# Planned transfer times, fewer reserved buffers, first transfers in pieces and a joint ending of the last two batches, in a fused four-layer graph network

## The chip, the core and the metric

The kernel runs on one NeuronCore of one Trainium2 chip. The metric is the device time of one execution, in microseconds (us), as the median of several executions. Each kernel was timed beside runs of the kernel before on the same chip. A ratio in this text is the mean time of one kernel's fast runs over that of the other's of the same rounds, so it is not quite the ratio of the medians that are quoted.

## The reference

For each of 32 batches there are 512 nodes of 128 features (`x`) and a dense 512x512 adjacency matrix (`adj`). Four residual graph layers follow each other, each behind a layer norm and a relu:

```python
h = relu(layernorm(x)); x = x + L0(h, adj)   # degree-normalised convolution, leaky relu
h = relu(layernorm(x)); x = x + L1(h, adj)   # in and out aggregation, node term, tanh
h = relu(layernorm(x)); x = x + L2(h, adj)   # four stacked layers, adj l2-normalised by rows / by columns
h = relu(layernorm(x)); x = x + L3(h, adj)   # message, aggregation, GRU-like gates
```

Everything is f32. PE (TensorE) does the products. All batches are independent, so work of one batch can fill the waits of another.

## The kernel before

The kernel describes each batch as a list of operations with an estimated duration, and a planner written in Python puts all operations of all batches into one order per engine. It is a list scheduler: an operation's key is its batch's due time minus the length of the chain that still follows it, and a buffer is only given to a younger batch if enough stay free for each older one (`kept`). The order is fixed when the kernel is built. On the chip each engine works strictly in that order.

```python
PERIOD = 20.0
...
    def order(self):
        ...
            o.tail = max([o.us + o.land] + [self.lag(o, n) + n.tail for n in o.next if n.batch == o.batch])
            o.key = (o.batch * PERIOD - o.tail, i)
        ...
                    older = item[1].batch - min(unfinished)
                    if any(len(free[x.kind]) < len([...]) + older * self.kept.get(x.kind, 0) for x in new):
                        held.append(item)
                        continue
...
    plan = Plan(sb, psum, {"bank": 8, "s2": 32, "s4": 6, "s8": 10}, {"bank": 1, "s2": 5, "s4": 1, "s8": 2})
...
        # transfers have fixed landing times in the plan
        op("SP", 0.1, lambda: nc.sync.dma_start(a.ap(), adj[b]...), [], [a], land=5.3)
```

The kind `s8` holds the large matrices: the adjacency `a`, its transpose `aT`, and a second copy `aT2` for the last layer, 1 MB each, and the last layer's gates `g`.

A norm goes through four engines. VectorE makes the moments, GpSimd the power -1/2, VectorE the bias `nb`, ScalarE the normalised relu `h`; PE then transposes `h`, and the next layer starts from that:

```python
            op("POOL", 0.35 + 0.17 * n, lambda: nc.gpsimd.tensor_tensor(inv..., v8..., neg_half..., op=ALU.pow), ...)
            op("DVE", 0.16, ... nb = -mean * inv ...)
            for c in range(NC):
                op("ACT", t_act(D, 2), ... h[c] = relu(inv[c] * x[c] + nb[c]) ...)
        ...
                op("PE", 0.11, lambda c=c: nc.tensor.transpose(ps..., h.ap()[:, c, :], ident), ...)
```

The l2 factors of the third layer are computed per node on partitions, written to DRAM (`bounce`) and read back as rows on all partitions (`rows`); eight multiplies on VectorE then scale `a` and `aT`.

## Time and profile before

| what | kernel before |
|---|---|
| time | 2486.97 us median of 3 (2486.08 to 2491.35) |
| span of the profiled run, mean granted clock | 2485.6 us, 0.992 |
| PE busy | 97% |
| a batch every (distance of adjacency loads) | 75.5 us |
| idle of PE between 300 and 2300 us, in the list of waits | 10.6 us |

One more view is needed later: PE's waits in the stretch from 300 to 2300 us (columns: who waited, for whom, us in total, times, the longest).

```profile
PE ps_agg L267 <- DVE sd L418: 8.7, 19, 0.6
```

This is nearly all that the list shows. It says that the aggregations of the third layer sometimes wait for VectorE's addition `sd`, and that PE hardly waits for anything else.

### The profile page before, as it was taken

The numbers are of one execution on the slowest core, as the hardware profiler recorded it, in microseconds if no ns is written. First come the engines' busy times: TensorE is split into PE (matmuls) and PEld (weight loads), VectorE is DVE, ScalarE is ACT, GpSimd is POOL, SyncE is SP. The second block draws the span as 40 slices with busy tenths as digits, with TensorE's granted clock in tenths as the row PEclk, the third lists the DMA queues.
The fourth block names the chain that finished last, engine by engine and source line by source line (L and its number), as shares of the span: only waits on it lengthen the run. The fifth ranks groups of instructions, "written<-read, shape, count | busy, mean of one in ns | idle before, by whom it ended". The sixth has DMA issues, their size and how long they took to land. (4 is left out here: it accounts for less than half of the span.)

```text
span 2485.6 us, 23454 instructions
## 1 busy us (share of the span) xinstructions
PE 2419.9 (97%) x8898; PEld 1466.4 (59%) x8898; DVE 1136.9 (46%) x2832; ACT 744.0 (30%) x1633; POOL 253.7 (10%) x199
## 2 busy tenths in 40 slices
PE   5899999999999999999999999999999999999997
PEld 4556566556566556566565665565665666655654
DVE  5334455444454444454444554444544444544343
ACT  3221333332333322333322333223333223333121
POOL 1110111100011101011101111010111010110000
PEclk8999999999999999999999999999999999999998
DMA  8011111111112111122111121111111121211000
GB/s 245 20 51 51 64 35 64 66 58 51 51 51 64 60 51 64 35 68 64 60 51 64 34 64 60 55 59 51 51 64 59 51 64 35 68 51 64 13 5 9
DMA packets 123489, 139.67 MB, mean 56 GB/s; under 512 B 36592, under 2 KB 69360, under 8 KB 123376
## 3 DMA queue, kind: packets, MB, share of 16 engines
q1 hardware_dynamic: 122368, 134.36, 16.9%
q10 hardware_dynamic: 1008, 3.81, 0.4%
q8 instruction: 70, 1.15, 0.2%
q14 instruction: 43, 0.35, 0.1%
HBM read 129.64 MB, written 8.52 MB: 56 GB/s over the span
## 5 line engine op out<-in xcount | busy, mean ns | idle before, releaser
L267 PE MATMUL ps_agg<-aT,sd 128*128 128x512 f32 x1024 | 504.5, 595 | 10.5 <-DVE sd L418 9.9
L267 PEld LDWEIGHTS ps_sd<-w_sb,f 128*128 128x128 f32 x1792 | 335.0, 190 | 252.9 <-issue 186.3
L267 PE MATMUL ps_sd<-w_sb,f 128*128 128x256 f32 x1792 | 482.0, 381 | 0.8 <-ACT f L541 0.8
L267 PE MATMUL ps_agg<-a,sd 128*128 128x512 f32 x1024 | 479.0, 592 | 0.0
L363 POOL TENSOR_TENSOR sc<-v,neg_half 128x4 f32<-128x4 f32 (+1 forms) x128 | 150.0, 1172 | 1933.7 <-DVE v L430 1046.8
L541 ACT ACTIVATE f<-ps_agg,cf_sb 128x512 f32<-128x512 f32 x128 | 88.0, 687 | 768.6 <-PE ps_agg L267 767.1
L418 DVE TENSOR_TENSOR sd<-ps_sd,rf_sb 128x512 f32<-128x512 f32 x256 | 175.9, 687 | 309.7 <-PE ps_sd L267 309.7
L267 PEld LDWEIGHTS ps_agg<-a,sd 128*128 128x128 f32 x1024 | 187.4, 190 | 195.8 <-issue 194.2
L375 ACT ACTIVATE h<-xr,nb,sc 128x128 f32<-128x128 f32 x384 | 158.1, 482 | 366.8 <-DVE nb L371 366.8
L267 PEld LDWEIGHTS ps_agg<-aT,sd 128*128 128x128 f32 x1024 | 189.4, 190 | 129.9 <-issue 92.8
L267 PE MATMUL ps_agg<-f,w_sb 128*128 128x512 f32 x448 | 228.7, 593 | 0.0
L429 DVE TENSOR_REDUCE stat<-a 128x4 f32<-128x2048 f32 x32 | 73.1, 2286 | 312.1 <-DMA a<-in_adj 312.1
L267 PE MATMUL ps_agg<-aT,rep 128*128 128x512 f32 x256 | 134.9, 609 | 4.2 <-DVE rep L481 4.2
L267 PE MATMUL ps_agg<-a,rep 128*128 128x512 f32 x256 | 132.0, 597 | 0.0
L267 PE MATMUL ps_agg<-aT,msg 128*128 128x512 f32 x256 | 124.0, 595 | 1.1 <-DVE msg L558 1.1
L525 DVE TENSOR_TENSOR a<-a,rows 128x512 f32<-128x512 f32 x128 | 116.5, 911 | 5.0 <-PE ps_agg L267 3.3
L575 DVE TENSOR_TENSOR g<-ps_gate,r_sb 128x512 f32<-128x512 f32 x128 | 79.5, 683 | 78.4 <-PE ps_gate L267 78.4
L267 PEld LDWEIGHTS ps_gate<-w_sb,hT 128*128 128x128 f32 x512 | 89.6, 193 | 36.0 <-issue 29.7
L267 PE MATMUL ps_gate<-w_sb,hT 128*128 128x256 f32 (+1 forms) x512 | 104.6, 329 | 0.0
L418 DVE TENSOR_TENSOR sd<-ps_sd,r_sb 128x512 f32<-128x512 f32 x64 | 44.2, 691 | 131.4 <-PE ps_sd L267 131.4
L456 DVE SCALAR_TENSOR_TENSOR z<-ps_lin,sc,r_sb 128x128 f32<-128x128 f32 x128 | 36.2, 343 | 143.4 <-PE ps_lin L267 143.3
L267 PE MATMUL ps_agg<-aT,h 128*128 128x256 f32 (+2 forms) x384 | 100.8, 384 | 0.0
(90 smaller groups left out, 2657.5 us busy)
## 6 DMA issues: line engine op xcount, KB each, us to landing
aT<-in_adjt SPq DMA_DIRECT2D x64, 1024.0 KB, 5.4
a<-in_adj SPq DMA_DIRECT2D x32, 1024.0 KB, 5.4
rows<-bounce SPq DMA_DIRECT2D x32, 512.0 KB, 4.4
x<-in_x SPq DMA_DIRECT2D x32, 256.0 KB, 2.8
out<-xo SPq DMA_DIRECT2D x32, 256.0 KB, 2.3
raw<-in_raw ACTq DMA_DIRECT2D x2, 768.0 KB, 9.6
w_sb<-in_w ACTq DMA_DIRECT2D x2, 448.0 KB, 6.8
r_sb<-in_brow ACTq DMA_DIRECT2D x1, 704.0 KB, 6.0
```

The costliest lines, as they stand in the source:

```text
L267: op("PE", t_mm(n), lambda: nc.tensor.matmul(out_of(ps.ap()), lhs(), rhs(), start=start, stop=stop), reads, [(ps, part) if part is not Non ...
L363: op("POOL", 0.35 + 0.17 * n, lambda: nc.gpsimd.tensor_tensor(inv.ap()[:, :n], v8.ap()[:, :n], neg_half[:, :n], op=ALU.pow), [v8, NH], [(i ...
L375: op("ACT", t_act(D, 2), lambda c=c: nc.scalar.activation(h.ap()[:, c, :], xin.ap()[:, c, :], AF.Relu, bias=nb.ap()[:, c:c + 1], scale=inv ...
L418: op("DVE", t_tt(N), lambda ps=ps, h=h: nc.vector.tensor_add(sd.ap()[:, 2 * h:2 * h + 2, :], ps.ap().rearrange("p (j v) -> p j v", j=2), a ...
L429: op("DVE", 2.2, lambda: nc.vector.tensor_reduce(stat.ap(), a.ap(), AX.X, ALU.add), [a], [stat])
L456: op("DVE", 0.28, lambda c=c: nc.vector.scalar_tensor_tensor(z.ap()[:, c * D:(c + 1) * D], ps0.ap()[:, c * D:(c + 1) * D], inv0.ap()[:, NC ...
L525: op("DVE", t_tt(N), lambda m=m, c=c, s=s: nc.vector.tensor_mul(m.ap()[:, c, :], m.ap()[:, c, :], rows.ap()[:, s, :]), [(m, {c}), rows], [ ...
L541: op("ACT", t_act(N, 1), lambda ps=ps, i=i, f_new=f_new: nc.scalar.activation(f_new.ap(), ps.ap(), AF.Tanh, bias=cf_sb[:, i:i + 1]), [ps, ...
L575: op("DVE", t_tt(N), lambda ps=ps, c=c: nc.vector.tensor_add(g.ap()[:, c, :], ps.ap(), r_sb[:, R_L3_G:R_L3_G + 4 * D]), [ps, RS], [(g, {c})])
```

## The change

Its intent, part by part:
1. The plan knows transfers by their size: each occupies its queue for kb/240 us and lands 1.3 us later, instead of fixed landing times.
2. The first transfers go in a fixed order (`rank`) and batch 0's matrices in four pieces, so that the first norm, row sums and aggregation can start early.
3. One `s8` buffer is kept per older batch instead of two.
4. `bounce` is stored with contiguous words; `rows` then comes back interleaved, and the multiplies read it with a stride of eight words.
5. Batch 31 is due 6 us after batch 30 instead of 20, so that the last two end together, and their gates go in chunks of 128 columns with two steps on GpSimd. The gate formula gets two ScalarE steps more and keeps six VectorE passes.

```diff
+ENDING = 6.0
+    RATE, TRANSFER = 240.0, 1.3
-    def op(self, engine, us, emit, reads=(), writes=(), land=0.0):
+    def op(self, engine, us, emit, reads=(), writes=(), kb=0.0, rank=None):
+        if kb:
+            o.us, o.land = max(us, kb / self.RATE), self.TRANSFER
-            o.key = (o.batch * PERIOD - o.tail, i)
+            due = o.batch * PERIOD if o.batch < B - 1 else (B - 2) * PERIOD + ENDING
+            o.key = (due - o.tail if o.rank is None else o.rank - 1e6, i)
-    plan = Plan(sb, psum, {... "s8": 10}, {"bank": 1, "s2": 5, "s4": 1, "s8": 2})
+    plan = Plan(sb, psum, {... "s8": 10}, {"bank": 1, "s2": 5, "s4": 1, "s8": 1})
...  (weights, biases and raw blocks: split, ranked, kb= instead of land=)
-        op("SP", 0.1, lambda: nc.sync.dma_start(a.ap(), adj[b]...), [], [a], land=5.3)
+        pieces = NC if b == 0 else 1
+        load(a, adj[b], 1024, 1)          # `pieces` transfers, rank 1 for batch 0
+        load(aT, adjt[b], 1024, 4)
...  (row sums and GpSimd's diagonal blocks follow the pieces of batch 0)
-        bounce, rows = buf("bounce", (2 * NC, P)), buf("s4", (P, 2, N), "rows")
+        bounce, rows = buf("bounce", (P, 2 * NC)), buf("s4", (P, P, 2, NC), "rows")
-        op("SP", 0.1, bounced, [inv], [bounce], land=4)
+        op("SP", 0.4, bounced, [inv], [bounce], kb=128)
+                    ... rows.ap()[:, :, s, :].rearrange("p n k -> p k n") ...   # stride of 8 words
+        at_end = b >= B - 2
+        side, side_engine = (nc.gpsimd, "POOL") if at_end else (nc.vector, "DVE")
+        w2 = 1 if at_end else NC
+            ... u, u, n = tanh(u), w = .5 - .5 z, q = .5 + .5 z, q *= h, q += x, n *= w, xo = q + n ...
```

## The prediction

> **What bounds the kernel now.** I read the page first: TensorE (PE) is busy for 97% of the span, in every slice but the first two and the last. Then I asked for PE's busy time in stretches (columns: stretch, its length, busy us and instructions, granted clock, DMA share, GB/s).
>
> ```profile
> span 2485.6 us, 23454 instructions
> PE 2419.9 (97%) x8898; PEld 1466.4 (59%) x8898; DVE 1136.9 (46%) x2832; ACT 744.0 (30%) x1633; POOL 253.7 (10%) x199
> ```
>
> ```profile
> 0.00:10.00 10.00, 0.00 (x0) 1.00 0.79 279
> 10.00:20.00 10.00, 6.17 (x32) 1.00 1.05 389
> 20.00:30.00 10.00, 7.41 (x36) 0.83 1.08 359
> 30.00:40.00 10.00, 7.37 (x37) 0.83 0.59 163
> 40.00:60.00 20.00, 14.11 (x41) 0.67 0.74 140
> 60.00:81.00 21.00, 14.67 (x57) 0.91 0.20 58
> ...
> 1300.00:2300.00 1000.00, 991.26 (x3651) 1.00 0.17 56
> 2300.00:2455.54 155.54, 155.23 (x571) 1.00 0.03 9
> 2455.54:2485.60 30.06, 13.65 (x56) 0.74 0.03 9
> ```
>
> See three kernels in one: a start of 81 us short of work and at a low clock, a long full middle, and a tail of 30 us that runs one batch's chain alone.
>
> How much PE work is there at full speed? In the timeline of the middle a product of 512 columns starts 0.86 us after the last, one of 256 after 0.43, of 128 after 0.22, a transpose after 0.11 to 0.12. One batch has 52, 40 and 28 such products, 3.5 us of mixed first-layer ones and 16 transposes: 44.7 + 17.2 + 6.2 + 3.5 + 2.0 = 73.6 us. With some 7 us of weight folding, 32 batches need 2362 us; 124 of the 2486 are lost. Where:
> - Start: PE's order and the timeline say that at 81 us it had done 33 us of work. Lost: 48.
> - End: from 2455.54 (last second-stack aggregation done) one batch's tail remains, 10.5 us of work in 30. Lost: 19.5.
> - Middle: the rest, 56, or 1.8 us a batch. The busy column hides most of it in pipelined ends; the distance between successive starts shows it. It agrees with the period: adjacency loads at 225.12 and 2263.61 us are 27 batches apart, 75.5 us each.
>
> The start, in the timeline: the first layer waits for data that all arrive together.
>
> ```profile
> 11.54 6.19 PE L267 MATMUL ps_fold<-raw 128*128 128x128 f32 x32 [11.54 <-DMA raw<-in_raw]
> 11.79 2.29 DVE L429 TENSOR_REDUCE stat<-a 128x4 f32<-128x2048 f32 x1 [4.56 <-DMA a<-in_adj]
> 18.66 0.87 DVE L347 BATCH_NORM_STATS2 bn<-x 128x6 f32<-128x128 f32 x4 [4.38 <-DMA x<-in_x]
> 45.20 3.78 PE L267 MATMUL ps_sd<-w_sb,hT 128*128 128x256 f32 x8 [0.68 <-ACT hT L386]
> 54.22 2.04 PE L267 MATMUL ps_agg<-aT,rep 128*128 128x512 f32 x2 [3.23 <-DVE rep L481]
> ```
>
> x, only 256 KB and the head of the chain, is used at 18.7 us, although a lone x load takes 2.6. Batch 0 reaches its second layer at 45.2. The last gates, in VectorE's timeline:
>
> ```profile
> 2474.15 2.48 DVE L575 TENSOR_TENSOR g<-ps_gate,r_sb 128x512 f32<-128x512 f32 x4 [7.93 <-PE ps_gate L267]
> 2477.33 0.69 DVE L583 SCALAR_TENSOR_TENSOR u<-g 128x512 f32<-128x512 f32 x1 [0.70 <-ACT g L580]
> ...
> 2481.68 0.69 DVE L590 TENSOR_TENSOR xo<-xr,dl 128x512 f32<-128x512 f32 x1
> ```
>
> PE ends at 2474.8; the span ends 10.8 later: 7.6 of VectorE and ScalarE in turn, 2.3 of output transfer, 0.9 of closing.
>
> **What the Trainium skill says.**
> 1. "TensorE: Matmul & The Clock Gate", section "What's actually happening": the array runs at half clock until it has been busy for about 3.4 us, and drops back after an idle window. The trace agrees: 0.67 to 0.91 granted in the hungry start, 0.74 in the tail, 1.00 between. So a wait costs more than its length, and a fuller tail is also a faster one.
> 2. "DMA: Bandwidth & Descriptors", section "Rules for kernel authors": a non-contiguous last dimension becomes one descriptor per element. The `bounce` store (4 KB as single words) takes 10.3 us median to land in the middle, against 2.3 for a 256 KB output: it agrees.
> 3. The same page, "Issuing engines are not separate DMA queues": all run on the same 16 engines and interleave. The window of 10 to 20 us shows 389 GB/s at a DMA share of 1.05: order and bytes decide, not queues.
> 4. "Vector Engine (DVE) Microarchitecture Reference", section "5.2 Measured stream behaviour on trn2 (trn3 not measured)": a source that hops at every element costs 1.73 ns a column instead of 1.05, up to 2.5 for small steps. No run so far shows it.
>
> **The change, part by part.**
>
> *First transfers.* Issued now: x, a in four pieces, small weights and biases beside them, then raw0, aT in four pieces, the rest. I lay them out at the measured 390 to 400 KB/us from about 2.2 us: x near 4 us; a with all before it is 1.45 MB, 6 us; raw0 7.8; aT 8.4 to 10.4; weights 12.8; the other raws 14.3 and 16.3; batch 1's a 19, aT 22.
>
> Chain of batch 0 with the trace's durations: last row sum 6.9, power on GpSimd (1.65) 8.9, two small VectorE steps 9.4, h from 9.9; the first aggregation behind the six raw0 folds (cold, 0.43 each), partly cold itself, about 10.8 to 16.5; copy and 4 products to 18.5; then z, y, residual, moments with fold copies between (5.5), power 1.1, h 1.7, transposes and copy 1: second layer at about **28.5** instead of 45.2. But PE has then done 10.7 us of work, not 15.5, since batch 1 comes later. Lost: 17.8 against 29.7, a gain of 12. From there to 81 us the old kernel lost another 18: cold products between 45 and 60, 3.2 for rep (a 2.28 us row sum of another batch stands before it), 2.6 for agg_in, 2.7 and 0.9 for the next norm. The new order keeps nearly all of these waits for a lone batch 0; I give it 5 us, mostly the row sum, which now comes before. **Start: -17.**
>
> *The middle.* The gate formula keeps six VectorE passes and adds two ScalarE ones, 1.2 us a batch on an engine 30% busy: nothing. `bounce` should land in about 2 us instead of 10, but no engine waited for rows: nothing. The eight multiplies by `rows` (680 and 691 ns) read every eighth word; by point 4 an estimate of 1.0 to 1.4 us each, some 4 us a batch on an engine 46% busy, and they precede the upd addition, which waits about 3.5 us after the aggregation anyway: up to 2 us hidden or spilt once.
>
> What matters is the new order (one kept buffer instead of two, other load times). I counted, in both kernels' PE order, the places where a result's first use follows its last producing product with less than 1.0 us of other work, about what an eviction takes: 5 a batch before (agg_in, agg_out, two hT, f), 2.5 after, total shortfall 0.74 and 0.36 us a batch. Times 31 that is 12 us; for slower multiplies and waits of norm chains, which this count does not see, I take a third off. **Middle: -8.**
>
> *The end.* Batch 31 is now due 6 us after batch 30 instead of 20. In the new order their last aggregations are 7 products apart; after the later one two tails remain, 20.5 us of work, where one (10.5) did. I walked it from that point, T0: f 1.8, h of batch 31 by 8.3, its message behind batch 30's gates at about 13.7, VectorE free after batch 30's four gate additions at 16, aggregation 16.4 to 19.8, gates to 23.3.
>
> Then the chunked ending: the order lists all four g additions, then 4 + 4 + 4 + 4 steps of 128 columns, so it is phased, not a true pipeline; ScalarE has 20 small pieces. By 0.22 to 0.28 us a step (the 128-column z steps: 1.13 for four) about 6 us, issue, 2 landing, closing: 9.3 instead of 10.8. End at T0 + 32.6, of which 20.5 is work: 12 lost instead of 19.5. **End: -7.5.**
>
> Sum: -17 - 8 - 7.5 = -32.5; 2487 - 32 = **2455 us**.
>
> **The rivals.**
> - *The end gives more, the start too: over 2%.* Needs 50 us, that is 40 of the 67.5 lost at both ends with 10 from the middle. For it: x can be there 14 us sooner and the tail was nearly idle. Against: every step of batch 0's chain between arrivals stays, alone and partly cold; two tails still hang on VectorE. Then 2430 to 2437.
> - *The plan breaks in the middle.* Rows' strided reads take 1.4 us, VectorE, which works in a fixed order, is late for the sd additions, whose slack is 1.07 to 1.28 us, and PE waits 0.3 to 0.5 more per batch instead of less: +10 to 15 us. For it: such a wait of 0.4 us per batch stands in the trace already. Against: in the new order no sd addition lies among the eight. Then 2470 to 2478.
> - *First transfers are hidden anyway.* If folds or the cold clock set the first 80 us, an earlier x is not worth 12 us: 2467. Against: folds are 7 us of 81.
>
> **Range and chances.** Start 10 to 24, middle -2 to 16, end 4 to 11; independent, they add to about 32 with 16 either way: 2439 to 2471. Over 2% faster is below 2437, just outside: 0.1. Over 2% slower needs +50 us, against three gains: 0.01.
>
> **What would show it.** Start: x statistics near 4 us, second-layer products near 28.5 (above 36 and the step is wrong); full busy windows from about 65. Middle: period 75.2, `rows` multiplies 1.0 to 1.4 us, bounce near 2 us, fewer waits for agg_in, agg_out, hT. End: last aggregation to end of span 32.6, PE end to end of span 9.3, clock near 1.0. The number is wrong if the period moves by more than 0.5 us in either direction, since it counts nearly thirty times.

## The result, and the profile after

The changed kernel took 2521.40 us (2520.69 to 2521.87, 4 runs) beside 2487.30 of the kernel before (2486.08 to 2491.35, 4 runs): a ratio of 1.0134 with a 95% interval of 1.0116 to 1.0152. It is 1.3% slower. That is still "within 2%", but far outside the predicted range of 2439 to 2471, and on the other side of the old time.

The page after, first lines (engine, busy us, share of the span, instructions):

```profile
PE 2422.4 (96%) x8898; PEld 1461.2 (58%) x8898; DVE 1218.1 (48%) x2855; ACT 786.8 (31%) x1719; POOL 363.0 (14%) x218
```

PE has the same number of products and the same busy time as before, in a longer span. VectorE has 81 us more and GpSimd 109 more. The same stretches as in the prediction, again with PE's busy time (columns: stretch, its length, busy us and instructions, granted clock, DMA share, GB/s):

```profile
10.00:20.00 10.00, 8.91 (x47) 1.00 1.04 400
20.00:30.00 10.00, 6.04 (x50) 0.97 1.01 329
...
40.00:60.00 20.00, 16.56 (x60) 0.84 0.61 204
60.00:81.00 21.00, 18.58 (x54) 0.84 0.24 76
...
1300.00:2300.00 1000.00, 972.11 (x3578) 1.00 0.17 55
...
2486.94:2519.90 32.96, 21.83 (x109) 0.92 0.06 17
```

The start is fuller, and the last row, which begins where the last second-stack aggregation is done, holds 21.83 us of work in 32.96 where the old tail held 13.65 in 30.06. Both ends do what they were meant to. The middle does not: 972 of 1000 us busy, where it had been 991. The steps of the start, in the timeline:

```profile
4.31 0.87 DVE L376 BATCH_NORM_STATS2 bn<-x 128x6 f32<-128x128 f32 x4 [4.31 <-DMA x<-in_x]
11.09 2.93 PE L276 MATMUL ps_fold<-raw 128*128 128x128 f32 x12 [11.09 <-DMA raw<-in_raw]
31.65 3.78 PE L276 MATMUL ps_sd<-w_sb,hT 128*128 128x256 f32 x8 [0.68 <-ACT hT L415]
39.71 2.05 PE L276 MATMUL ps_agg<-aT,rep 128*128 128x512 f32 x2 [2.95 <-DVE rep L516]
```

Batch 0 reaches its second layer 13.6 us sooner and the next aggregation 14.5 us sooner than before. PE's waits in the middle (300 to 2300 us, columns as above):

```profile
PE ps_t L412 <- ACT h L404: 29.1, 46, 0.9
PE ps_agg L276 <- DVE rep L516: 17.9, 25, 0.9
PE ps_agg L276 <- DVE sd L447: 4.9, 15, 0.3
```

Two waits have grown from nothing and from one wait of 0.8 us: the transposes for the normalised `h`, and the second layer's aggregation for `rep`. The old one, for `sd`, has become smaller.

**What a batch loses.** The list of waits and the busy columns miss whatever lies inside the modelled end of a product. So take the distances between successive starts on PE over the 27 batches between two loads of `a` (225.12 to 2263.61 us before, 207.6 to 2293.0 after), and subtract for each instruction the distance at which such instructions follow each other when nothing holds them up: 0.43 us for 512 columns (a product counts as two instructions), 0.32 for 384, 0.215 for 256, 0.111 for 128 and 0.11 for a transpose. What is left is lost time, here in us per batch by what comes next:

| lost, us per batch | before | after |
|---|---|---|
| at the transposes of `h` (before, inside or behind them) | 0.65 | 2.39 |
| at the aggregation of `rep` | 0.10 | 0.91 |
| at third-layer aggregations (`sd`) | 0.61 | 0.33 |
| at products of `hT` | 0.47 | 0.07 |
| everything else | 0.29 | 0.23 |
| sum | 2.12 | 3.93 |
| a batch every, from the adjacency loads | 75.50 | 77.24 |

The work of a batch is 73.4 us before and 73.3 after (the edges of the stretch are not quite alike), so the difference of the sums, 1.81, is that of the periods, 1.74, to within 0.1. So the change lost about 50 us in the middle (28 full batches by 1.74 are 49), and gained some 15 at both ends. Told apart by norm, the 0.65 of before lies wholly at the norm behind the first layer. After, all three transposed norms lose: about 1.1 us behind the first layer, 1.2 behind the second layer's update and 0.5 behind the third layer (these overlap a little with other rows).

**Where the new waits come from.** The chain in front of a late transpose, in the timeline of all engines after. PE's last update product ends at 1334.35, where its next one starts:

```profile
1321.49 1.27 POOL L472 TENSOR_TENSOR diag<-aT,ident 128x512 f32<-128x512 f32 x1 [5.01 <-ACT rep L513]
1321.66 1.40 DVE L514 TENSOR_SCALAR rep<-rep 128x512 f32<-128x512 f32 x1
...
1324.20 1.10 PE L276 MATMUL ps_agg<-aT,rep 128*128 128x512 f32 x2 [0.91 <-DVE rep L516]
...
1334.55 0.69 DVE L529 TENSOR_TENSOR u<-ps_upd,r_sb 128x512 f32<-128x512 f32 x1 [0.55 <-PE ps_upd L276]
1335.27 0.63 ACT L531 ACTIVATE y<-u 128x512 f32<-128x512 f32 x1 [3.35 <-DVE u L529]
1335.94 0.69 DVE L533 TENSOR_TENSOR xr<-xr,y 128x512 f32<-128x512 f32 x1
1336.66 0.87 DVE L376 BATCH_NORM_STATS2 bn<-xr 128x6 f32<-128x128 f32 x4
...
1338.16 1.01 POOL L392 TENSOR_TENSOR sc<-v,neg_half 128x4 f32<-128x4 f32 x1 [2.65 <-DVE v L379]
1339.40 1.65 ACT L404 ACTIVATE h<-xr,nb,sc 128x128 f32<-128x128 f32 x4 [2.00 <-DVE nb L400]
1339.95 0.71 PE L412 MATMUL ps_t<-ident,h 128*128 128x128 f32 x2 [0.69 <-ACT h L404]
```

Read it from 1334.35: update added, tanh, residual, moments, power, `h`, and the transpose at 1339.95, that is 5.6 us of chain. PE's other work in that time (four msg products of 0.111, ten instructions of 0.43) is 4.74, so PE stands for 0.86. The first three lines show the other wait: VectorE's scaling of `rep` takes 1.40 us, where the same instruction 1.4 us later takes 0.39, because GpSimd's diagonal addition runs beside it; the aggregation of `rep` waits for 0.91.

The same place in PE's timeline of the kernel before:

```profile
1156.34 1.02 PE L383 MATMUL ps_t<-ident,h 128*128 128x128 f32 x3
1157.19 1.02 PE L267 MATMUL ps_agg<-aT,msg 128*128 128x512 f32 x2
...
1173.60 1.02 PE L267 MATMUL ps_agg<-f,w_sb 128*128 128x512 f32 x2
...
1182.26 0.60 PE L383 MATMUL ps_t<-ident,h 128*128 128x128 f32 x4
```

Here the last update product ends at 1173.60 and the transposes stand at 1182.26, 8.66 us later. The chain has 3 us to spare. Over the whole middle, this distance is 8.66 to 8.88 us before, and 5.6 and 5.9 in turn after. The first two lines show a hidden wait of before: three transposes, 0.33 us of work, take 0.85 until the next start, though no idle time is noted in the brackets.

### The profile page after: what moved, and what is told of

The parts are those of the page before. It is cut to its first block, busy times and chain, and to the rows that moved or that the text cites. A ratio compares the mean times of both kernels' runs of the same rounds, so it can differ in the third digit from the quotient of the medians.

```text
span 2519.9 us, 23554 instructions
## 1 busy us (share of the span) xinstructions
PE 2422.4 (96%) x8898; PEld 1461.2 (58%) x8898; DVE 1218.1 (48%) x2855; ACT 786.8 (31%) x1719; POOL 363.0 (14%) x218
## 5 line engine op out<-in xcount | busy, mean ns | idle before, releaser
L276 PE MATMUL ps_sd<-w_sb,f 128*128 128x256 f32 x1792 | 466.5, 381 | 0.7 <-ACT f L415 0.7
L544 POOL TENSOR_TENSOR inv<-stat,neg_half 128x8 f32<-128x8 f32 x32 | 140.8, 4400 | 139.6 <-DVE stat L543 127.8
L560 DVE TENSOR_TENSOR a<-a,rows 128x512 f32<-128x512 f32 x128 | 151.7, 1186 | 1.1 <-PE ps_agg L276 1.1
L412 PEld LDWEIGHTS ps_t<-ident,h 128*128 128x128 f32 x384 | 52.6, 140 | 152.9 <-ACT h L404 130.5
L560 DVE TENSOR_TENSOR aT<-aT,rows 128x512 f32<-128x512 f32 x128 | 138.4, 1081 | 0.0
L621 ACT ACTIVATE g<-g 128x512 f32<-128x512 f32 (+1 forms) x68 | 40.9, 604 | 306.8 <-DVE g L611 306.8
L412 PE MATMUL ps_t<-ident,h 128*128 128x128 f32 x384 | 92.5, 297 | 40.7 <-ACT h L404 36.9
```

The source lines that it names most:

```text
L276: op("PE", t_mm(n), lambda: nc.tensor.matmul(out_of(ps.ap()), lhs(), rhs(), start=start, stop=stop), reads, [(ps, part) if part is not Non ...
L412: op("PE", 0.11, lambda c=c: nc.tensor.transpose(ps.ap()[:, c * P:(c + 1) * P], h.ap()[:, c, :], ident), [(h, {c}), ID], [(ps, {c})])
L544: op("POOL", 1.7, lambda: nc.gpsimd.tensor_tensor(inv.ap(), stat.ap(), neg_half, op=ALU.pow), [stat, NH], [inv])
L560: op("DVE", t_tt(N), lambda m=m, c=c, s=s: nc.vector.tensor_mul(m.ap()[:, c, :].rearrange("p (k n) -> p k n", k=NC), m.ap()[:, c, :].rearr ...
L621: op("ACT", t_act(cols), lambda s=s: nc.scalar.activation(g.ap()[:, s, :2 * D], g.ap()[:, s, :2 * D], AF.Tanh, scale=0.5), [(g, part)], [( ...
```

## The experiments

Twelve kernels ran. I state the theory as it stood in the end first; the expectations show what was held when. **Theory:** the two planner settings, counted transfer times and one kept `s8` buffer, produce an order in which norm chains end later than the work laid beside them, and the layout of rows and the end are harmless. **Rivals:** VectorE is slowed by the strided reads; or the counted times alone, or the kept buffer alone, are to blame; or the new start is what disturbs the middle.

### Is it the strided reads?

`e1_contiguous_factors` is the changed kernel, reading rows as if they were contiguous. It is wrong, with the same order on every engine.

```diff
-  rows.ap()[:, :, s, :].rearrange("p n k -> p k n")
+  rows.ap().rearrange("p n s c -> p (n s c)")[:, s * N:(s + 1) * N].rearrange("p (k n) -> p k n", k=NC)
```

> The changed kernel with the same instruction order on every engine; only the eight multiplies by rows read the factors contiguously (wrong factors, so a wrong result on purpose). Multiplies theory (the slower strided multiplies make VectorE late and PE waits): the multiplies fall from about 1.08 to 0.68 us, the period falls from 77.5 to about 75.5, time about 2470 to 2480 us. Order theory (one kept buffer instead of two gives PE an order that reaches the transposes and the rep products too early): multiplies fall as well, but the period stays above 77 and the time is 2508 to 2521 us.

Measured: 2515.04 us (2514.14 to 2516.36), ratio to before 1.0106 [1.0091, 1.0121]. The multiplies fell from 1.08 to 0.69 us, the time by 6. The transposes still wait for 25.9 us and `rep` for 17.9.

`e2_strided_in_before` is the kernel before with the new layout of `bounce` and `rows` alone; the compute engines keep their order.

```diff
-  bounce, rows = buf("bounce", (2 * NC, P)), buf("s4", (P, 2, N), "rows")
+  bounce, rows = buf("bounce", (P, 2 * NC)), buf("s4", (P, P, 2, NC), "rows")   # and the reads to match
```

> The kernel before with only the new layout of bounce and rows: same order on PE, VectorE, ScalarE and GpSimd. Multiplies theory: 1.08 us each and some 40 to 50 us slower, 2525 to 2540 us. Order theory: multiplies 1.08 us, the bounce store lands in 2 us instead of 10, the period stays 75.5 and the time is 2483 to 2497 us.

Measured: correct, 2484.40 us (2482.36 to 2486.63) beside 2490.01, ratio 0.9983 [0.9968, 0.9998]; multiplies at 1.08 us, a batch every 75.5 us. In an order with room, the strided reads cost nothing. In the new order they cost 6 of the 50 us.

### Which planner setting?

`e3_kept_two`: the changed kernel with two kept `s8` buffers.

```diff
-  {"bank": 1, "s2": 5, "s4": 1, "s8": 1}
+  {"bank": 1, "s2": 5, "s4": 1, "s8": 2}
```

> The changed kernel with one number put back: two kept large buffers per older batch instead of one. Order theory: the middle's extra 50 us go and the gains of both ends stay, period about 75.5, time 2462 to 2480 us. Multiplies theory: the multiplies are as slow as before, so 2510 to 2525 us.

Measured: correct, 2517.22 us (2516.59 to 2518.28), ratio 1.0115 [1.0100, 1.0130]. The order theory's forecast (2462 to 2480) missed: one kept buffer alone was not the cause. The number lies in the range of the multiplies theory, but e1 and e2 had excluded that. Undoing this one part gains next to nothing, but the kernel is now slow in another way. The loads of `a` in the timeline of SP:

```profile
1140.47 0.37 SPq L366 DMA_DIRECT2D a<-in_adj  x1
1200.42 0.38 SPq L366 DMA_DIRECT2D a<-in_adj  x1
1294.97 0.37 SPq L366 DMA_DIRECT2D a<-in_adj  x1
```

They are 60 and 94.5 us apart in turn. The plan has fallen into a cycle of two batches. The loss moved too: PE's waits for `sd` are 37.6 us in the stretch 300 to 2300, and by starts 1.8 us per batch are lost at third-layer aggregations and 1.4 at the transposes (26 batches).

`e4_kept_two_old_rates`: two kept, and the old fixed times in the plan except for the first loads (these change the order only, no instruction).

```diff
+  if land is not None: o.us, o.land = 0.1, land
   # x 2.8, a and aT 5.3 for b > 0; aT2 5.3, bounce and rows 4, out 2.3 for every b
-  {... "s8": 1}
+  {... "s8": 2}
```

> As e3, and the plan's transfer times after batch 0 put back to the old fixed landings. By a count on the instruction order PE's middle is then the order of the kernel before. Order theory: period 75.5, 2465 to 2480 us; if e3 is worse than this by over 10 us, the new transfer rates have a share of the loss. Multiplies theory: 2510 to 2525 us.

Measured: correct, 2459.87 us (2459.04 to 2461.21) beside 2490.01, ratio 0.9884 [0.9868, 0.9901]. It beats both kernels, and lies 5 us below the range of the order theory. A batch every 75.01 us; the middle's windows and waits:

```profile
1300.00:2300.00 1000.00, 995.00 (x3699) 1.00 0.17 56
```

```profile
PE ps_agg L278 <- DVE sd L449: 8.6, 23, 0.6
```

Busy 995 where the changed kernel had 972, and the only wait left is the old one. By starts a batch loses 1.64 us: 0.36 at the transposes, 0.28 at `rep`, 0.58 at `sd`. The new start and the new end are still in this kernel, and so are the strided reads, so none of them spoils the middle by itself.

`e5_old_rates_one_kept` closes the square: old times, one kept buffer.

```diff
   # e4 with
-  {... "s8": 2}
+  {... "s8": 1}
```

> The changed kernel with one kept buffer (as it is), but the plan's transfer times for all batches but the first set back to the fixed ones of before. Completes the square of kept buffers by transfer times (2521 with new times and one kept, 2517 new and two, 2460 old and two). Theory A (one kept buffer spaces the batches so tightly in each chain that results arrive too late, whatever the transfer times): 2505 to 2522 us, waits of the transposes for h near 29 us in the stretch 300 to 2300, work near 973 per 1000 us. Rival B (the counted transfer times alone spoil the order, one kept buffer is harmless with the old ones): 2455 to 2470 us, work near 993 per 1000, waits only for sd.

Measured: correct, 2512.90 us (2512.25 to 2513.66) beside 2494.32, ratio 1.0075 [1.0058, 1.0092]. The transposes wait for 25.7 us again. The distance from the last update product to its transpose has a median of 5.60 us, against 8.88 in e4. So one kept buffer packs the chains too tightly with either set of times.

`e8_load_times_old_two_kept`: two kept, old fixed times for the loads of `x`, `a`, `aT` and `aT2` only.

```diff
   # e4 without the old times of bounce, rows and out
-  op("SP", 0.4, bounced, [inv], [bounce], kb=128, land=4)
+  op("SP", 0.4, bounced, [inv], [bounce], kb=128)
```

> The changed kernel with two kept buffers, the counted transfer times for bounce, rows and output, but the old fixed times for the loads of x, a and aT in all batches but the first. Theory A (with two kept buffers it is the loads' planned landing that tips the plan into a cycle of two batches): even a loads 75.0 us apart, work near 994 per 1000, 2456 to 2466 us. Rival (the other transfers' times, 0.4 to 2 us off, tip it as well): a loads alternating near 60 and 94 us, 2505 to 2520.

Measured: correct, 2461.38 us (2461.20 to 2462.03) beside 2494.32, ratio 0.9869 [0.9854, 0.9884]; a batch every 75.01 us. With two kept buffers, setting back the loads' times alone is enough.

| time us (ratio to before) | one kept | two kept |
|---|---|---|
| counted transfer times | 2521.4 (1.0134), the change | 2517.2 (1.0115) |
| old fixed times for the loads | 2512.9 (1.0075), all transfers | 2459.9 (0.9884) all, 2461.4 (0.9869) loads only |

Neither setting can be called the culprit alone. Each is enough to spoil the order, in its own way, and only with both undone is the middle good.

### Are the norm chains out of slack?

`e6_cheap_power_after` and `e7_cheap_power_before`: in the changed kernel and in the kernel before, the power in the norms becomes a subtraction of the same shape, with the same order on every engine. Their outputs are wrong, which doesn't matter for the times.

```diff
-  nc.gpsimd.tensor_tensor(inv..., v8..., neg_half..., op=ALU.pow)
+  nc.gpsimd.tensor_tensor(inv..., v8..., v8..., op=ALU.subtract)
```

> The changed kernel, same order of instructions on every engine, with GpSimd's power in the norms (1.01 us for 128x4, 1.66 for 128x8) replaced by a subtraction of the same shape; results wrong on purpose (all norms become 0), the powers of the rows stay. A norm chain becomes about 0.8 us shorter. Theory A (in the new order three chains a batch end later than the work laid beside them, so what is cut from a chain comes back whole until the shortfall is gone): waits of the transposes for h fall from 29 us to under 8 in the stretch 300 to 2300, and the time by 25 to 45 us to 2476 to 2496. Rival B (the loss is in the stream of multiplies, in VectorE's lateness or in PE itself, the waits at the transposes only show it): under 12 us, 2509 to 2521.

Measured: 2457.47 us (2456.07 to 2458.16) beside 2494.32, ratio 0.9852 [0.9837, 0.9867]. The instruction fell from 1.01 to 0.20 us. The gain is 64 us by the medians and 70 by the ratios (the kernel before was slower in this call), more than the 25 to 45 of theory A, and the waits at the transposes are nearly gone:

```profile
PE ps_t L412 <- ACT h L404: 1.8, 7, 0.4
```

By starts, the loss at the transposes fell from 2.39 to 0.78 us per batch, and that at `rep` nearly stayed, 0.80. A batch takes 75.17 us instead of 77.24. So the chains were out of slack, as the theory says.

> Control: the same replacement in the kernel before, same order on every engine, wrong on purpose in the same way. Theory A: there the transposes do not wait for h, so the middle gains nothing; start and end have six such steps of 0.8 us on their paths, so 2 to 8 us: 2479 to 2485. Rival B (a cheaper norm helps any order): 2450 to 2470.

Measured: 2450.36 us (2449.35 to 2451.43), ratio 0.9824 [0.9810, 0.9839]. I expected at most 8 us, and it is 44. My control failed, and the reading behind it was wrong: the kernel before does wait for its norms, only not where the list of waits shows it. By starts, it lost 0.65 us at the transposes and 0.61 at `sd`; with the cheap power nothing at either. A batch takes 74.19 us instead of 75.50. What joins the two is a line of VectorE's groups (columns: busy us, mean ns | idle before, released by), first of the kernel before, then of e7:

```profile
L371 DVE SCALAR_TENSOR_TENSOR nb<-mv,sc 128x4 f32<-128x4 f32 x128 | 20.8, 163 | 103.6 <-POOL sc L363 102.5
```

```profile
L371 DVE SCALAR_TENSOR_TENSOR nb<-mv,sc 128x4 f32<-128x4 f32 x128 | 20.9, 163 | 26.7 <-POOL sc L363 25.6
```

VectorE, whose order is fixed, stands for 0.8 us in the mean before each of 128 norms until GpSimd's power is done, and an `sd` addition behind it starts that much later. That this is how the waits for `sd` arose is my reading; what is shown is that both went away together.

Against each other the two runs say: of the 1.74 us per batch that the change lost, 2.07 - 1.31 = 0.76 hang on GpSimd's power in particular.

### Is the collision at `rep` real?

`e12_diag_without_reads`: the changed kernel, with GpSimd's addition of the identity to the diagonal blocks replaced by a fill at the same place. Its output is wrong, which doesn't matter for the time.

```diff
-  nc.gpsimd.tensor_tensor(diag.ap()[:, k:k + n, :], blocks, ident..., op=ALU.add)
+  nc.gpsimd.memset(diag.ap()[:, k:k + n, :], 0.01)
```

> The changed kernel with GpSimd's addition of the identity to the diagonal blocks of aT (128x512, two sources, 1.2 to 2.1 us) replaced by a fill with a constant at the same place in GpSimd's order; wrong on purpose; the order on PE, VectorE, ScalarE and SP is the same from the fourth batch on. Theory A (VectorE's scaling of rep, 0.42 us alone, takes 1.40 because this addition runs beside it on GpSimd, and the rep aggregation waits for it every second batch): scaling of rep back near 0.42 to 0.6 us in the mean (0.64 now), wait of the rep aggregation from 17.9 us to under 6 in the stretch 300 to 2300, 12 to 24 us faster: 2497 to 2509. Rival B (the chain from the sd eviction to rep is too short of time without any collision): the wait stays above 12 us and the time within 6 us of 2521. Rival C (the fill holds VectorE up just as well): scaling of rep still 0.6 us in the mean, no gain.

Measured: 2507.43 us (2507.16 to 2508.07) beside 2488.42, ratio 1.0076 [1.0060, 1.0093], so 14 us faster than the change. The scaling of `rep` takes 0.46 us in the mean instead of 0.64 (300 to 2300 us). The wait went down to 7.0 us, not quite under the 6 that I had set:

```profile
PE ps_agg L276 <- DVE rep L516: 7.0, 13, 0.5
```

Theory A holds for the larger part: 76.71 us a batch instead of 77.24, and 0.53 lost at `rep` instead of 0.91. Some of this wait is there without the collision.

### What are the start and the end worth?

Three kernels, all from e4, in 5 rounds (before: 2488.07).

`e9_no_new_end`: without both parts of the new end.

```diff
-  due = o.batch * PERIOD if o.batch < B - 1 else (B - 2) * PERIOD + ENDING
+  due = o.batch * PERIOD
-  at_end = b >= B - 2
+  at_end = False
```

> The mended kernel (old transfer times, two kept buffers: 2460 in an earlier call) without either part of the new end: batch 31 due 20 us after batch 30 as before, its gates whole. What is left against the kernel before is the new start, the new layout of rows and the new gate formula, on nearly the same order in the middle. Theory (three separate terms, start and end of the prediction real): start 10 to 17 us, the rest nothing, so 2470 to 2478 us, and the mended kernel's end is worth 10 to 18. Rival (the start gives only what PE has ahead at 81 us, near 9): 2476 to 2480. Rival 2 (the gain lies in the middle): within 5 us of 2460.

Measured: correct, 2466.54 us (2465.44 to 2468.04), ratio 0.9912 [0.9899, 0.9926]. That is 21.5 us faster than before without any new end, and lies between the theories. From the traces: its first adjacency load of the middle is at 217.5 where before had it at 225.1 in a like order, so the start gives 7.6; 27 batches then take 2024.1 us instead of 2038.5, so the middle gives 14.4.

`e10_whole_gates_at_end`: joint end, but whole gates (only the second pair of lines above).

> The mended kernel with only the chunked ending of the last two batches taken out (gates whole, as in all other batches); the last two still end together. Prediction's step: the chunked ending is worth 1.5 us (9.3 against 10.8 from the end of PE to the end). Theory: 2460 to 2463 us. Rival (chunks save a real pipeline's worth): 2464 to 2468. Rival 2 (the small pieces cost as much as they save): 2457 to 2460.

Measured: correct, 2458.76 us (2458.27 to 2459.32), ratio 0.9881 [0.9867, 0.9894]. The joint end is worth 7.8 us (2466.54 to 2458.76). The chunks are worth nothing: e4, which has them, has the ratio 0.9884, with overlapping intervals. From the end of PE's last product to the end of the span it is 9.7 us whole, 10.0 in chunks. This is below the 2460 to 2463 of the prediction's step and in the range of its second rival, that the small pieces cost as much as they save. As a correct kernel it is the best, tied with e4 and e8.

`e11_last_batch_due_20`: chunks, but the last batch due as before (only the first pair).

> The mended kernel with only the due time of the last batch set back to 20 us after the one before it (chunked gates kept). Prediction's step: two tails beside each other lose 12 us where one lost 19.5, less the 1.5 of the chunks, so 6 us: 2464 to 2468. Rival (two tails hang on VectorE, joint end worth nothing): 2458 to 2462. Rival 2 (worth more since the tail runs at a higher clock): 2469 to 2475.

Measured: correct, 2468.42 us (2467.31 to 2470.70), ratio 0.9919 [0.9905, 0.9932], just above the 2464 to 2468 of the prediction's step. It is not told apart from whole gates with the same due time (2466.54; the intervals overlap), so here too the chunks gain nothing. The trace shows one wait for `sd`, of 1.67 us, while batch 30's small pieces run:

```profile
2433.22 1.98 PE L278 MATMUL ps_agg<-aT,sd 128*128 128x512 f32 x4 [1.67 <-DVE sd L449]
```

## Why the prediction was wrong

**Start, -17: right in kind, half in size.** The x statistics came at 4.31 us, as laid out. What followed did not arrive at the 390 to 400 KB/us that had been laid out from 2.2 us on: the trace after has 171 GB/s from 2 to 4 us, 197 from 4 to 6, and over 400 only then. The last piece of `a` landed at 9.2 us instead of 6, raw0 at 11.0 instead of 7.8. The folds of raw0 start at 11.09, the first aggregation at 14.24 instead of 10.8, and the second layer at 31.65 instead of 28.5, late by the same 3 us. Counted by starts, PE had done 33.5 us of work at 81 us before, as the prediction says, and 41.9 after: a gain of 8, and e9 gives 7.6. The full windows were to begin at about 65; but 60 to 81 us still had a clock of 0.84 and 18.58 of 21 us busy. Up to the second layer the step held in the main: by then 20.0 us were lost (31.65 less 11.7 of work) against 29.7 before (45.20 less 15.5), a gain of 9.7 where 12 was predicted. The part that failed is "I give it 5 us" for what follows: from there to 81 us the new order lost 19.1 us, the old one 17.7, so 1.4 were given back instead of 5 gained.

**Middle, -8: wrong in sign, and the reason for the whole miss.** The step that failed is "I counted ... the places where a result's first use follows its last producing product with less than 1.0 us of other work", followed by "waits of norm chains, which this count does not see, I take a third off". The waits that it did count fell about as it said (0.38 us a batch): those for `hT` alone from 0.47 to 0.07. Those for `sd`, which it had left to a rival, fell too, from 0.61 to 0.33. But the chains that it did not see pass through four engines and take 5.6 us, and they are where a batch loses most: 0.65 at the transposes before, 2.39 after. Taking a third off a gain was no substitute for counting, for each norm, the distance from the products that feed it to its transposes; behind the update it is 8.66 us in one order and under 6 in the other. Both orders lay ready when the prediction was written.

The prediction also overlooked the collision at `rep` (about half of the 0.81 us that were added there, e12), though it stands on GpSimd and VectorE in the order. Its remaining terms were sound: the new gate formula costs nothing that shows (e9 has it, though not alone), rows' multiplies take 1.08 us, inside 1.0 to 1.4 (the upper end had no ground in the page for a single hopping source), and cost 6 us at most (e1) or nothing (e2), `bounce` lands in 1.4 us (median), against the 2 that were guessed.

**The rivals.** "The plan breaks in the middle" was the right heading with the wrong wait: VectorE's lateness at `sd`. It expected 10 to 15 us; the loss was 50. Its counter-argument, that no sd addition lies among the eight multiplies, holds in the trace, and `sd` waits became fewer. The prediction gave this rival no chance of its own, and even its range, 2470 to 2478, lay below the old time. Had it been about any chain that returns to PE, it would have deserved more.

**End, -7.5: right.** From the last second-stack aggregation to the end of the span: 32.8 us from its modelled end, predicted 32.6. The sum is 7.8 in e10 against e9. Its split was not right: the joint end gave the 7.8, not 6, and the chunks nothing, not 1.5. From PE's end to the end of the span it is 10.0 us, not 9.3. The g additions for the last batch:

```profile
2509.20 2.48 DVE L611 TENSOR_TENSOR g<-ps_gate,r_sb 128x512 f32<-128x512 f32 x4 [2.23 <-PE ps_gate L276]
...
2515.61 0.88 DVE L638 TENSOR_TENSOR xo<-q,n 128x128 f32<-128x128 f32 x4
```

As foreseen, all four g additions come first and the chunks follow in phases: there is no pipeline, and the four last `xo` still end at 2516.5, 7.3 us after the first g.

**The sum in measured terms**: start -8, middle +49, end -8, together +33; measured +34. With a sound order (e4) it is start -8, middle -14, end -8, together -30; measured 2459.9 by a ratio of 0.9884, that is -29. The predicted 2455 would have been nearly right for the change's parts, had its planner settings been other ones, but in part by luck: the start gave half of its term and the middle nearly twice.

**What stays open.** That one kept buffer tightens the chains is shown (e4 against e5). Why it does is only argued: with fewer buffers held back for older batches, a younger batch gets its matrices sooner and stands closer behind. About 0.3 us of the 1.74 per batch is not assigned: 0.76 hang on the power, 0.53 on the collision, 0.16 on the strided reads (77.24 to 77.08 in e1), if these may be added. Why the middle of e4, e8 and e9 is 0.5 us a batch better than that of the kernel before, with the same planner settings, was not tested; by starts they lose less at the transposes (0.36 for 0.65) and at `hT` (0.19 for 0.47), and more at `rep` (0.28 for 0.10). Why the first transfers were slow until 6 us is open too.

## What to carry to other kernels

A planner's order is a result to be measured, not an improvement by itself: truer transfer times gave a worse order here, and two settings had to be right together. Count, for each chain that returns to the bounding engine, its length in the trace against the work laid beside it, the longest chains first; a list of waits that shows nothing does not mean slack, and start-to-start distances do. The 44 us that a cheaper power in the norms gives even the kernel before are the next thing to look for in this kernel; it needs a correct replacement, which was not found here.

## What the Trainium skill lacked or had wrong

- "SBUF — State Buffer", section "SBUF: two separate sides", says that VectorE and GpSimd share one port pair as an exclusive lock, and that the loser "fully blocks". The traces agree: VectorE's scaling of `rep` takes 1.40 us beside GpSimd's addition and 0.39 to 0.43 alone. The page tells of one instruction that blocks another. Here GpSimd's power for the rows took 6.44 us, ending 1.5 us after a row of VectorE multiplies had ended, where it takes 1.64 to 1.68 otherwise; over the whole run its mean is 4.40 us after and 1.68 before, and 2.04 when the multiplies read contiguously (e1); with the strided reads in the old order (e2) the median stays 1.64. How long a row of instructions can keep GpSimd out is missing.
- "Vector Engine (DVE) Microarchitecture Reference", section "5.2 Measured stream behaviour on trn2 (trn3 not measured)": for one source that hops at every element it has a row for steps of 4 KiB, 1.73 ns a column. A row for one source in small steps is missing. Here one source in steps of eight words took the multiplies from 0.69 to 1.08 us for 512 columns, 2.1 ns a column all told.
- No page that I found gives the time of a power on GpSimd: 1.01 us for 128x4 elements and 1.65 for 128x8, against about 0.2 for a subtraction of either shape (e6, e7). It was worth 44 us in the kernel before and 64 to 70 in the changed one.
